# Gathered rows in four PSUM banks, sums three ticks behind, and edge steps set apart in a graph network kernel

## The chip, the cores and the metric

The kernel runs on one core of a Trainium2 chip. The metric is the device time of one execution in microseconds. Three runs of the kernel before gave 4328.02, 4320.78 and 4327.1 us; the median is 4327.1 us. A separate execution under the hardware profiler took 5199.93 us. Instruction times below come from that execution.

## What is computed

Two graph layers over 12,500 nodes with 64 features and 200,000 edges, sorted by `dst`. The first layer is two mean aggregations with weights, the second a small network per edge with a mean by `src`:

```python
def _sage_conv(x, src, dst, Wl, Wr, b):
    agg = jax.ops.segment_sum(x[src], dst, num_segments=N)
    cnt = jax.ops.segment_sum(jnp.ones((src.shape[0],), x.dtype), dst, num_segments=N)
    mean = agg / jnp.maximum(cnt, 1.0)[:, None]
    return mean @ Wl.T + b + x @ Wr.T
...
h = jnp.maximum(_layernorm(x, axis=-1), 0.0)
x = x + conv2(relu(conv1(h)))
h = jnp.maximum(_layernorm(x, axis=-1), 0.0)
# second layer, per edge (senders = src, receivers = dst)
inp = jnp.concatenate([h[senders], h[receivers], edge_attr_64], axis=-1)
msg = jax.nn.relu(inp @ W1 + b1) @ W2 + b2
x = x + _segment_mean(msg, senders, N)
```

`conv1` and `conv2` stand for `_sage_conv` with the two sets of weights.

## The kernel before

Gather and scatter are matrix products. The nodes are cut into 49 blocks of 256, the edges into 49 x 49 = 2401 cells by the block of their two ends, each cell padded to 128 places. A gather multiplies a one-hot matrix (`turned`, 128 places by 256 nodes in two halves) with a block's table of node rows; a sum multiplies another one-hot matrix (`hot`) with the gathered rows. A table keeps each value in three bf16 pieces, so a row has 3 x 64 = 192 columns, and 193 with the count.

The stages, in order:

1. `features` (to about 114 us of the profiled execution): layer norm of the inputs.
2. `cells` (to about 857 us): places the edges of a block in their cells, block by block.
3. The two convolutions (L812 to L825, to about 3713 us, with a drain of some 14 us): a loop over 2 x 601 ticks, each of four cells or the odd one left over.
4. The last stage (L831 on): per-edge messages and their mean, eight cells a tick.

**A tick of the convolutions.** `Line` keeps a list of generators. `line.tick(new)` adds a generator and advances each by one step, the oldest first. `some_cells` (L769) is the generator of four cells: in its first step eight gather products (L775) into `got`, one `hot` on VectorE (L639), and one ScalarE copy (L782) of 768 columns from PSUM to bf16 `rows`; then two yields; then the eight sum products (L664) into `acc`. So TensorE's queue holds, tick after tick, the sums of two ticks ago and then the gathers of this one. When the last cell of a block has been summed, the same generator goes on with `conv` (L700): a ScalarE copy of the sums (L703) in the same step, then the mean and the reassembled own rows on VectorE (L707 to L715), two transposes (L719), a copy (L721), the weights (L725), bias (L727), and `after_conv1` or `after_conv2`, which writes the next tables.

**PSUM** has eight banks. `psum_x` holds two for everything named `pX`, which `conv`, `after_conv2`, `final` and `edge_terms` share. `sums_ps` holds two for `acc` and four for `got`: two buffers of two banks, each for four cells.

**Beside the ticks** runs `edge_terms` (L321), the part of the second layer that needs only the edge attributes. It works in 209 units of mostly four transposes: transpose (L353), ScalarE copy (L355), product with the weights (L361, each recorded as two), ScalarE copy (L364), and up to eight indirect scatters on GpSimd (L369) into the tables `terms` in memory. It is a generator too. `Beside` advances it by counted time: each tick counts 0.37 or 0.375 us a cell, each step costs 10.4/6 us. In the cell stage it is advanced from block 18 on, 2.4 us at each of five places a block. A full unit is six steps: transpose and copy; product; copy and two scatters; two scatters; two; two.

**`tb`** is the table of the second convolution. As `after_conv2` computes the receivers' table for the last stage, it stores each block to `b_mem` (L767), since `tb` is still being gathered; the last two blocks go to `tb` at once. The list `again` (L812) loads `tb` back seven blocks at a time, once they have been gathered for the last time.

The order of every engine's queue is that in which the program writes it (a manual schedule); each engine runs its queue in order.

Of the kernel before, what the change touches and what calls it, by code (L numbers as in the profile page):

```python
# [9 lines left out]
FT = mybir.dt.float32  # L10
# [104 lines left out]
def fast_path(  # L115
# [205 lines left out]
    def edge_terms(work, psum):  # L321

        loads = []
        for q in (*range(BJ - 3), BJ - 1, BJ - 3, BJ - 2):
            blocks = range(q * J, min(q * J + J, NB))
            step = 3 if len(blocks) == J else 4
            loads += [(blocks, t0, min(step, TG - t0)) for t0 in range(0, TG, step)]

        def load(blocks, t0, m):
            n = len(blocks)  # L330
            e = work.tile([P, J, 3, 2 * D], FT, name="edges")
            ev = e.rearrange("p j c d -> p (j c) d").rearrange("p (a c) d -> p a c d", a=n if n == J else 1)
            for i, B in enumerate(blocks):
                s = nc.sync.value_load(begin_i[0:1, B:B + 1], min_val=0, max_val=E - WIN)
                a = edge[bass.ds(s, WIN)].rearrange("(p t) d -> p t d", t=T)
                nc.sync.dma_start(ev[:, i, 0:m].rearrange("p c d -> p (c d)"),
                                  a[:, 2 * t0:2 * (t0 + m)].rearrange("p t d -> p (t d)"))
            return ev

        ahead = load(*loads[0])  # L340
        for at, (blocks, t0, m) in enumerate(loads):
            n = len(blocks)
            ev = ahead

            if n == J:
                units = [[(i, t0 + c, ev[:, i, c]) for i in range(n)] for c in range(m)]
            else:
                units = [[(0, t0 + c, ev[:, 0, c]) for c in range(m)]]
            for u, unit in enumerate(units):
                k = len(unit)  # L350
                pt = psum.tile([P, 4, P], FT, name="pX", bufs=2)
                for c, (_, _, a) in enumerate(unit):
                    nc.tensor.transpose(pt[:, c], a, ident)  # L353
                et = work.tile([P, 4, P], FT, name="edges_t")
                nc.scalar.copy(et[:, :k], pt[:, :k])  # L355
                if u == 0 and at + 1 < len(loads):
                    ahead = load(*loads[at + 1])
                yield
                pm = psum.tile([P, 4, 2, D], FT, name="pX", bufs=2)
                for c in range(k):  # L360
                    nc.tensor.matmul(pm[:, c], et[:, c], we, start=True, stop=True)  # L361
                yield
                o = work.tile([P, 4, 2, D], FT, name="terms_o", bufs=4)
                nc.scalar.copy(o[:, :k], pm[:, :k])  # L364
                for h in range(2):
                    for c, (i, tg, _) in enumerate(unit):
                        B = blocks[i]
                        t = 2 * tg + h
                        nc.gpsimd.indirect_dma_start(  # L369
                            out=terms[B % J][:], out_offset=bass.IndirectOffsetOnAxis(  # L370
                                ap=pos[:, B, t:t + 1], axis=0),
                            in_=o[:, c, h], in_offset=None,
                            bounds_check=EROWS - 1, oob_is_err=False)
                        if c % 2 == 1:
                            yield

    class Beside:

# [314 lines left out]
    psum = ctx.enter_context(tc.tile_pool(name="sums_ps", bufs=2, space=bass.MemoryType.PSUM))  # L693
    sums = Sums(psum)
    layers = ExitStack()
    work = layers.enter_context(tc.tile_pool(name="layers", bufs=2))
    next_rows = rows_with_one(work)
    line = Line()

    def conv(layer, table, w, b, finish, B, acc):  # L700

        v = work.tile([P, 2, W3], FT, name="sums")
        nc.scalar.copy(v, acc[:, :, :W3])  # L703
        yield
        m = work.tile([P, 2, 2, D], FT, name="both")
        t = table[:, B]
        nc.vector.tensor_add(m[:, :, 1], t[:, :, 0:D], t[:, :, D:2 * D])  # L707
        nc.vector.tensor_add(m[:, :, 1], m[:, :, 1], t[:, :, 2 * D:])
        nc.vector.tensor_add(m[:, :, 0], v[:, :, 0:D], v[:, :, D:2 * D])
        nc.vector.tensor_add(m[:, :, 0], m[:, :, 0], v[:, :, 2 * D:D3])  # L710
        if layer == 0:
            c = work.tile([P, 2], FT, name="cnt")
            nc.vector.tensor_scalar(c, v[:, :, D3], 1.0, None, op0=OP.max)
            nc.vector.reciprocal(rcnt[:, B], c)
        nc.vector.tensor_mul(m[:, :, 0], m[:, :, 0], bc(rcnt[:, B], D))  # L715
        yield
        pt = psum_x.tile([P, 4, P], FT, name="pX", bufs=2)
        for h in range(2):
            nc.tensor.transpose(pt[:, h], m[:, h].rearrange("p a d -> p (a d)"), ident)  # L719
        ct = work.tile([P, 2, P], FT, name="both_t")  # L720
        nc.scalar.copy(ct, pt[:, :2])  # L721
        yield
        po = psum_x.tile([P, 8, D], FT, name="pX", bufs=2)
        for h in range(2):
            nc.tensor.matmul(po[:, h], ct[:, h], w, start=True, stop=True)  # L725
        o = work.tile([P, 2, D], FT, name="conv")
        nc.vector.tensor_add(o, po[:, :2], rows(b, 2))  # L727
        yield
        yield from finish(B, o)
# [6 lines left out]
    def after_conv2(B, o):  # L736
# [9 lines left out]
        yield from layernorm_relu(work, h, v, 2)  # L746
        yield
        nc.sync.dma_start(of_block(x2_mem, B), v)
        pt = psum_x.tile([P, 4, P], FT, name="pX", bufs=2)
        nc.tensor.transpose(pt[:, 0], h.rearrange("p h d -> p (h d)"), ident)  # L750
        ht = work.tile([P, P], FT, name="h2_t")
        nc.scalar.copy(ht, pt[:, 0])
        yield
        po = psum_x.tile([P, 4, P], FT, name="pX", bufs=2)
        nc.tensor.matmul(po[:, 0:2], ht, wsr, start=True, stop=True)
        ab = work.tile([P, 2, 2, D], FT, name="ab", bufs=3)
        nc.scalar.copy(ab[:, 0], po[:, 0:2, :D])
        nc.vector.tensor_add(ab[:, 1], po[:, 0:2, D:], rows(bias[2], 2))
        yield
        last = B >= NB - 2  # L760
        b = tb[:, B] if last else work.tile([P, 2, D3], BF, name="b_out", bufs=3)
        for _ in zip_longest(three(work, ta[:, B], ab[:, 0], nc.vector.tensor_sub),
                             three(work, b, ab[:, 1], nc.vector.tensor_sub)):
            yield
        yield
        if not last:
            nc.sync.dma_start(of_block(b_mem, B), b)  # L767

    def some_cells(layer, t, c0, a, z):  # L769
        n = z - a  # L770
        table = (ta, tb)[layer]
        p = psum.tile([P, 2, 512], FT, name="got")
        for c in range(n):
            for h in range(2):
                nc.tensor.matmul(p[:, c // 2, c % 2 * D3:(c % 2 + 1) * D3],  # L775
                                 t[:, h, (a - c0 + c) * S:(a - c0 + c + 1) * S],
                                 table[:, (a + c) % NB, h], start=h == 0, stop=h == 1,
                                 skip_group_check=True)
        o = hot(work, dcol[:, even(a, z)], 4)
        g = next_rows()  # L780
        if n == G:
            nc.scalar.copy(g[:, :, :D3].rearrange("p (a c) d -> p a c d", c=2),  # L782
                           p[:, :, :2 * D3].rearrange("p a (c d) -> p a c d", c=2))
        else:
            for c in range(n):
                nc.scalar.copy(g[:, c, :D3], p[:, c // 2, c % 2 * D3:(c % 2 + 1) * D3])
        yield
        yield
        B = sums.add(o, g, a, z)
# [19 lines left out]
                    pass  # L809


    again = [(s, min(s + CH, NB - 2)) for s in range(0, NB - 2, CH)]  # L812
    todo = [(layer, *p) for layer in range(2) for p in parts(G)]
    for (layer, c0, c1, part), t, coming in ahead(
            todo, lambda p: wait_rows(work, "srow", srow_b, p[1], p[2]),
            lambda p, r: turned(work, "turned", r, p[2] - p[1])):
        for a, z in part:
            line.tick(some_cells(layer, t, c0, a, z))
            next(coming, None)
            beside.passed((z - a) * (0.37, 0.375)[layer])  # L820
            while layer and again and z - (CELLS - NB) >= again[0][1]:
                B0, B1 = again.pop(0)
                nc.sync.dma_start(tb[:, B0:B1],
                                  b_mem[B0 * BLK:B1 * BLK].rearrange("(b p h) d -> p b h d", p=P, h=2))
    line.finish()  # L825
    beside.rest()
    layers.close()
    terms_in.close()


    work = ctx.enter_context(tc.tile_pool(name="last", bufs=2))  # L831

    def final(K, acc):
        v = work.tile([P, 2, W3], FT, name="sums")
# [14 lines left out]
        nc.vector.tensor_mul(o, rows(bias[3], 2), bc(c[:, 2], D))  # L849
        nc.vector.tensor_add(o, o, xv)  # L850
        yield
        pt = psum_x.tile([P, 4, P], FT, name="pX", bufs=2)
        nc.tensor.transpose(pt[:, 0], m.rearrange("p h d -> p (h d)"), ident)
        mt = work.tile([P, P], FT, name="m_t")
        nc.scalar.copy(mt, pt[:, 0])
        yield
        po = psum_x.tile([P, 8, D], FT, name="pX", bufs=2)
        nc.tensor.matmul(po[:, 0:2], mt, wo, start=True, stop=True)
        yield
        nc.vector.tensor_add(o, o, po[:, 0:2])  # L860
# [76 lines left out]
    for (c0, c1, part), (ts, td), coming in ahead(  # L937
            list(parts(G3)), lambda p: (wait_rows(work, "srow", srow_k, p[0], p[1]),
                                        wait_rows(work, "drow", drow_k, p[0], p[1])), turned_both):
        for n, (a, z) in enumerate(part):  # L940
            p = psum.tile([P, G3, 2 * D], FT, name="got")
            line.tick_behind(messages(e, p, ts, td, c0, a, z))
            for _ in range(2):
                next(coming, None)
# [266 lines left out]
```

## Time and profile before

| | |
|---|---|
| median of three runs | 4327.1 us |
| profiled execution | 5199.93 us |
| its span | 5197.9 us |
| mean granted TensorE clock | 0.896 |

The profiled execution is 873 us longer than the median. Shares within it are read stage by stage, and a sum made in it does not carry over to the median one to one.

| engine | busy, us | share of the span |
|---|---|---|
| TensorE products (PE) | 4002.0 | 77% |
| TensorE weight loads (PEld) | 3699.5 | 71% |
| VectorE (DVE) | 3406.1 | 66% |
| GpSimd (POOL) | 2641.4 | 51% |
| ScalarE (ACT) | 2418.3 | 47% |

A group line names the source line, engine, operation and tiles; after the bar stand busy time, the mean of one in ns, the engine's idle time just before the group, and what ended most of it. TensorE overlaps consecutive products, so one product lasts some 250 ns in the records while the next starts about 83 ns later.

### The profile page before, as it was taken

Reading aid. Unit: us, or ns where it says so; the run is one execution under the profiler, and the core shown is the slowest. Engines: PE = TensorE matmul, PEld = TensorE weight load, DVE = VectorE, ACT = ScalarE, POOL = GpSimd, SP = SyncE. Lnnn points to the kernel's source line nnn. Section 1 sums busy time; section 2 is a strip of 40 time slices with the busy share of each in tenths; the row PEclk is TensorE's granted clock in tenths of the full one; section 3 lists DMA queues with packets and bytes.
Section 4 is the critical chain, followed back from the end, with each engine's and each line's share of the span. In section 5 each row is a group of like instructions: output and inputs, shape, how many; then the busy total and the mean of one; then the engine's idle time right before and its main releaser. Section 6 shows DMA issues by size and latency. Waiting matters only on the chain.

```text
span 5197.9 us, 123211 instructions
## 1 busy us (share of the span) xinstructions
PE 4002.0 (77%) x50387; PEld 3699.5 (71%) x50387; DVE 3406.1 (66%) x6079; ACT 2418.3 (47%) x4487; POOL 2641.4 (51%) x2300
## 2 busy tenths in 40 slices
PE   0785674778777877777777776777799999999897
PEld 0454453777777777677777775777788988888897
DVE  6784662555445544455555554555799999999997
ACT  2010112444444444444444443444566776676676
POOL 2047876555445554455455535555255555555554
PEclk9665766999889999899899988999899999999999
DMA  6941212233223222223233232322445544554453
GB/s 230 346 150 33 55 39 71 89 95 93 87 78 95 91 90 78 86 87 103 82 97 95 89 96 76 97 88 86 157 161 177 176 169 165 177 170 165 165 178 113
DMA packets 309518, 620.81 MB, mean 119 GB/s; under 512 B 74402, under 2 KB 158630, under 8 KB 308864
## 3 DMA queue, kind: packets, MB, share of 16 engines
q1 hardware_dynamic: 247572, 557.98, 32.5%
q0 software_dynamic: 53312, 51.36, 3.4%
q8 instruction: 395, 6.47, 0.5%
q10 hardware_dynamic: 8060, 3.53, 0.3%
q14 instruction: 179, 1.47, 0.1%
HBM read 465.04 MB, written 150.96 MB: 119 GB/s over the span
## 4 chain that ended last, share of the span: by engine, by line
PE 49%; issue 14%; DVE 10%; another core or an unknown queue 7%; POOL 7%; ACT 6%; DMA 2%; SPq 0%; POOLq 0%; ACTq 0%; DVEq 0%
PE acc L664 18%; PE got L775 11%; PE got L884 8%; POOL terms L369 7%; PE got L885 4%; ACT rows L782 4%; PE pX L361 3%; DVE turned_d L630 2%; DVE turned L630 1%; DVE hot L639 1%; PE pX L353 1%; DVE y L890 1%; DMA terms<-terms_o,pos 1%; PE pX L725 1%
## 5 line engine op out<-in xcount | busy, mean ns | idle before, releaser
L369 POOL DMA_INDIRECT terms<-terms_o,pos x1666 | 1834.7, 1101 | 1718.7 <-ACT terms_o L364 593.6
L782 ACT CAST rows<-got 128x768 bf16<-128x768 f32 x1200 | 958.4, 801 | 1443.5 <-PE got L775 740.1
L664 PEld LDWEIGHTS <-hot 128*128 128x128 bf16 x12006 | 1110.8, 103 | 360.3 <-issue 332.4
L664 PE MATMUL acc<-rows,hot 128*128 128x193 bf16 x9604 | 1087.7, 259 | 269.7 <-ACT rows L782 229.5
L897 POOL TENSOR_TENSOR hidden<-hidden 128x512 f32<-128x512 f32 (+1 forms) x602 | 771.6, 1282 | 752.9 <-ACT hidden L894 642.7
L630 DVE TENSOR_SCALAR turned<-srow,nid 128x2048 bf16<-128x2048 bf16 (+1 forms) x906 | 749.7, 842 | 334.1 <-PE got L775 139.0
L639 DVE TENSOR_TENSOR hot<-dcol,local 128x1024 bf16<-128x1024 bf16 x1202 | 801.0, 683 | 156.3 <-remote 75.9
L775 PEld LDWEIGHTS <-turned 128*128 128x128 bf16 x9604 | 863.5, 102 | 29.3 <-issue 20.9
L884 PE MATMUL got<-tb,turned_d 128*128 128x128 bf16 x4802 | 755.0, 223 | 83.5 <-DVE turned_d L630 83.5
L884 PE MATMUL got<-ta,turned 128*128 128x128 bf16 x4802 | 743.8, 222 | 23.4 <-DVE y L891 15.9
L885 PE MATMUL got<-tb,turned_d 128*128 128x64 bf16 x4802 | 686.1, 195 | 0.0
L885 PE MATMUL got<-ta,turned 128*128 128x64 bf16 x4802 | 677.8, 195 | 0.0
L775 PE MATMUL got<-ta,turned 128*128 128x192 bf16 x4802 | 531.1, 256 | 9.0 <-issue 8.4
L775 PE MATMUL got<-tb,turned 128*128 128x192 bf16 x4802 | 526.2, 255 | 6.8 <-issue 6.6
L361 PE MATMUL pX<-we,edges_t 128*128 128x128 f32 x1666 | 290.1, 327 | 311.8 <-ACT edges_t L355 203.6
L884 PEld LDWEIGHTS <-turned_d 128*128 128x128 bf16 x4802 | 449.1, 100 | 99.1 <-DVE turned_d L630 95.4
L905 ACT ACTIVATE hot_a<-every,less 128x256 bf16<-128x256 bf16 x1200 | 507.1, 493 | 0.0
L361 PEld LDWEIGHTS pX<-we,edges_t 128*128 128x128 f32 x1666 | 250.9, 230 | 342.4 <-ACT edges_t L355 222.3
L884 PEld LDWEIGHTS <-turned 128*128 128x128 bf16 x4802 | 449.9, 99 | 35.5 <-DVE y L891 27.2
L885 PEld LDWEIGHTS <-turned_d 128*128 128x128 bf16 x4802 | 447.0, 99 | 0.0
L885 PEld LDWEIGHTS <-turned 128*128 128x128 bf16 x4802 | 445.1, 99 | 0.0
L906 ACT ACTIVATE hot_a<-hot_a 128x1024 bf16<-128x1024 bf16 x300 | 317.1, 1057 | 9.5
(207 smaller groups left out, 4944.8 us busy)
## 6 DMA issues: line engine op xcount, KB each, us to landing
srow<-srow_b SPq DMA_DIRECT2D x300, 512.0 KB
terms<-zero SPq DMA_DIRECT2D x96, 832.0 KB
srow<-srow_k SPq DMA_DIRECT2D x150, 512.0 KB
drow<-drow_k SPq DMA_DIRECT2D x150, 512.0 KB
terms_in<-terms SPq DMA_DIRECT2D x147, 384.0 KB
edges<-in_edge_attr_dram SPq DMA_DIRECT2D x240, 192.0 KB
terms<-terms_o,pos POOLq DMA_INDIRECT x1666
terms_in<-terms SPq DMA_DIRECT2D x49, 416.0 KB
```

What stands on the lines that cost most here:

```text
L361: nc.tensor.matmul(pm[:, c], et[:, c], we, start=True, stop=True)
L369: nc.gpsimd.indirect_dma_start(out=terms[B % J][:], out_offset=bass.IndirectOffsetOnAxis(ap=pos[:, B, t:t + 1], axis=0), in_=o[:, c, h], i ...
L630: nc.vector.tensor_scalar(o[:, h, :n * S], r[:, :n * S], nid[:, h:h + 1], None, op0=OP.is_equal)
L639: nc.vector.tensor_tensor(o[:, :n], cols.rearrange("p (g c) -> p g c", c=2).unsqueeze(2).to_broadcast([P, n, 2 * P, 2]), local.rearrange(" ...
L664: nc.tensor.matmul(self.acc[B][:, h, :W3], lt, r[:, c, 0:W3], start=k + h == 0, stop=k == NB - 1 and h == 1, skip_group_check=True)
L775: nc.tensor.matmul(p[:, c // 2, c % 2 * D3:(c % 2 + 1) * D3], t[:, h, (a - c0 + c) * S:(a - c0 + c + 1) * S], table[:, (a + c) % NB, h], s ...
L782: nc.scalar.copy(g[:, :, :D3].rearrange("p (a c) d -> p a c d", c=2), p[:, :, :2 * D3].rearrange("p a (c d) -> p a c d", c=2))
L884: nc.tensor.matmul(p[:, c], lt, rt[:, 0:2 * D], start=i == 0, stop=False, skip_group_check=True)
L885: nc.tensor.matmul(p[:, c, 0:D], lt, rt[:, 2 * D:], start=False, stop=i == 3, skip_group_check=True)
L897: nc.gpsimd.tensor_sub(w[:, :n, (i + 1) * D:(i + 2) * D], w[:, :n, j], upper(w)[:, :n, j])
L905: nc.scalar.activation(q[:, c - k], every, AF.Abs, bias=less[(a + c) // NB][:, (a + c) % NB:(a + c) % NB + 1])
L906: nc.scalar.activation(q[:, :n - k], q[:, :n - k], AF.Relu, bias=1.0, scale=-2.0)
```

## The change

- `some_cells` takes a pair of cells at a time: four gather products into a tile of one bank, then a ScalarE copy of 384 columns. The tile has four buffers, in a pool of its own (`gather_ps`), closed after the convolutions.
- A third yield stands before the sums, and `hot` gets five buffers instead of four.
- `conv` begins with a yield, so its ScalarE copy of the sums comes one tick after them.
- `pX` keeps one bank for the node side; `edge_terms` has its own, `pE`.
- In `edge_terms` each operation has a step of its own: transpose; copy; nothing; product; nothing; copy. The scatters form a generator `scatter`, of which two are issued in each of the four middle steps of the next unit.
- The reload of `tb` is decided as the program is written: which blocks have been gathered for the last time, which are stored, which are present.
- The last stage's `got` gets a pool of its own with the same two buffers; its operations stay.

```diff
+        def scatter(o, blocks, unit):
+            for h in range(2):
+                for c, (i, tg, _) in enumerate(unit):
+                    B = blocks[i]
+                    t = 2 * tg + h
+                    nc.gpsimd.indirect_dma_start(
+                        out=terms[B % J][:], out_offset=bass.IndirectOffsetOnAxis(
+                            ap=pos[:, B, t:t + 1], axis=0),
+                        in_=o[:, c, h], in_offset=None,
+                        bounds_check=EROWS - 1, oob_is_err=False)
+                    if c % 2 == 1:
+                        yield
+        before = iter(())
...
-                pt = psum.tile([P, 4, P], FT, name="pX", bufs=2)
+                pt = psum.tile([P, 4, P], FT, name="pE")
                 for c, (_, _, a) in enumerate(unit):
                     nc.tensor.transpose(pt[:, c], a, ident)
-                et = work.tile([P, 4, P], FT, name="edges_t")
-                nc.scalar.copy(et[:, :k], pt[:, :k])
                 if u == 0 and at + 1 < len(loads):
                     ahead = load(*loads[at + 1])
                 yield
-                pm = psum.tile([P, 4, 2, D], FT, name="pX", bufs=2)
+                et = work.tile([P, 4, P], FT, name="edges_t")
+                nc.scalar.copy(et[:, :k], pt[:, :k])
+                next(before, None)
+                yield
+                next(before, None)
+                yield
+                pm = psum.tile([P, 4, 2, D], FT, name="pE")
                 for c in range(k):
                     nc.tensor.matmul(pm[:, c], et[:, c], we, start=True, stop=True)
+                next(before, None)
                 yield
+                next(before, None)
+                yield
+                for _ in before:
+                    pass
                 o = work.tile([P, 4, 2, D], FT, name="terms_o", bufs=4)
                 nc.scalar.copy(o[:, :k], pm[:, :k])
-                for h in range(2):
...
+                before = scatter(o, blocks, unit)
+                yield
+        for _ in before:
+            pass
...
+    gather = layers.enter_context(tc.tile_pool(name="gather_ps", bufs=4, space=bass.MemoryType.PSUM))
...
     def conv(layer, table, w, b, finish, B, acc):
 
+        yield
         v = work.tile([P, 2, W3], FT, name="sums")
         nc.scalar.copy(v, acc[:, :, :W3])
...
-        pt = psum_x.tile([P, 4, P], FT, name="pX", bufs=2)
+        pt = psum_x.tile([P, 4, P], FT, name="pX")
...
-        last = B >= NB - 2
+
+        last = gathered[0] > B
         b = tb[:, B] if last else work.tile([P, 2, D3], BF, name="b_out", bufs=3)
+        if last:
+            present.add(B)
...
             nc.sync.dma_start(of_block(b_mem, B), b)
+            stored.add(B)
...
     def some_cells(layer, t, c0, a, z):
         n = z - a
         table = (ta, tb)[layer]
-        p = psum.tile([P, 2, 512], FT, name="got")
-        for c in range(n):
-            for h in range(2):
-                nc.tensor.matmul(p[:, c // 2, c % 2 * D3:(c % 2 + 1) * D3],
...
-        o = hot(work, dcol[:, even(a, z)], 4)
         g = next_rows()
-        if n == G:
-            nc.scalar.copy(g[:, :, :D3].rearrange("p (a c) d -> p a c d", c=2),
-                           p[:, :, :2 * D3].rearrange("p a (c d) -> p a c d", c=2))
...
+        for c in range(0, n, 2):
+            m = min(2, n - c)
+            p = gather.tile([P, 512], FT, name="got")
+            for i in range(c, c + m):
+                for h in range(2):
+                    nc.tensor.matmul(p[:, (i - c) * D3:(i - c + 1) * D3],
+                                     t[:, h, (a - c0 + i) * S:(a - c0 + i + 1) * S],
+                                     table[:, (a + i) % NB, h], start=h == 0, stop=h == 1,
+                                     skip_group_check=True)
+            nc.scalar.copy(g[:, c:c + m, :D3], p[:, :m * D3].rearrange("p (c d) -> p c d", c=m))
+        o = hot(work, dcol[:, even(a, z)], 5)
+        yield
         yield
         yield
         B = sums.add(o, g, a, z)
...
-    again = [(s, min(s + CH, NB - 2)) for s in range(0, NB - 2, CH)]
+    gathered, stored, present = [0], set(), set()
+
+    def again():
+        new = [B for B in range(gathered[0]) if B in stored and B not in present]
+        if new and (len(new) >= CH or not line.all):
+            B0 = new[0]
+            B1 = next(B for B in range(B0, NB + 1) if B not in new or B == B0 + CH)
+            nc.sync.dma_start(tb[:, B0:B1],
+                              b_mem[B0 * BLK:B1 * BLK].rearrange("(b p h) d -> p b h d", p=P, h=2))
+            present.update(range(B0, B1))
+            return True
...
-            while layer and again and z - (CELLS - NB) >= again[0][1]:
-                B0, B1 = again.pop(0)
...
+            if layer:
+                gathered[0] = max(z - (CELLS - NB), 0)
+                again()
     line.finish()
+    while again():
+        pass
...
+    gather = ctx.enter_context(tc.tile_pool(name="last_ps", bufs=2, space=bass.MemoryType.PSUM))
...
-            p = psum.tile([P, G3, 2 * D], FT, name="got")
+            p = gather.tile([P, G3, 2 * D], FT, name="got")
```

More of the change, by code (lines that the diff above doesn't have):

```diff
@@ L358, in edge_terms @@
                 yield
-                pm = psum.tile([P, 4, 2, D], FT, name="pX", bufs=2)
+                et = work.tile([P, 4, P], FT, name="edges_t")
[5 more added lines that the diff above has]
+                pm = psum.tile([P, 4, 2, D], FT, name="pE")
                 for c in range(k):
                     nc.tensor.matmul(pm[:, c], et[:, c], we, start=True, stop=True)
+                next(before, None)
                 yield
+                next(before, None)
+                yield
+                for _ in before:
+                    pass
                 o = work.tile([P, 4, 2, D], FT, name="terms_o", bufs=4)
                 nc.scalar.copy(o[:, :k], pm[:, :k])
-                for h in range(2):
[L366 to L375, printed above, removed]
+                before = scatter(o, blocks, unit)
+                yield
+        for _ in before:
+            pass
     class Beside:
@@ L722, in conv @@
         yield
-        po = psum_x.tile([P, 8, D], FT, name="pX", bufs=2)
+        po = psum_x.tile([P, 8, D], FT, name="pX")
         for h in range(2):
@@ L748, in after_conv2 @@
         nc.sync.dma_start(of_block(x2_mem, B), v)
-        pt = psum_x.tile([P, 4, P], FT, name="pX", bufs=2)
+        pt = psum_x.tile([P, 4, P], FT, name="pX")
         nc.tensor.transpose(pt[:, 0], h.rearrange("p h d -> p (h d)"), ident)
@@ L753, in after_conv2 @@
         yield
-        po = psum_x.tile([P, 4, P], FT, name="pX", bufs=2)
+        po = psum_x.tile([P, 4, P], FT, name="pX")
         nc.tensor.matmul(po[:, 0:2], ht, wsr, start=True, stop=True)
@@ L771, in some_cells @@
         table = (ta, tb)[layer]
-        p = psum.tile([P, 2, 512], FT, name="got")
-        for c in range(n):
-            for h in range(2):
[L775 to L778, printed above, removed]
-        o = hot(work, dcol[:, even(a, z)], 4)
-        g = next_rows()
-        if n == G:
-            nc.scalar.copy(g[:, :, :D3].rearrange("p (a c) d -> p a c d", c=2),
-                           p[:, :, :2 * D3].rearrange("p a (c d) -> p a c d", c=2))
-        else:
-            for c in range(n):
-                nc.scalar.copy(g[:, c, :D3], p[:, c // 2, c % 2 * D3:(c % 2 + 1) * D3])
+        g = next_rows()
+        for c in range(0, n, 2):
[10 more added lines that the diff above has]
+        yield
         yield
@@ L820, in fast_path @@
             beside.passed((z - a) * (0.37, 0.375)[layer])
-            while layer and again and z - (CELLS - NB) >= again[0][1]:
-                B0, B1 = again.pop(0)
-                nc.sync.dma_start(tb[:, B0:B1],
-                                  b_mem[B0 * BLK:B1 * BLK].rearrange("(b p h) d -> p b h d", p=P, h=2))
+            if layer:
+                gathered[0] = max(z - (CELLS - NB), 0)
+                again()
     line.finish()
+    while again():
+        pass
+    assert present == set(range(NB))
     beside.rest()
@@ L851, in final @@
         yield
-        pt = psum_x.tile([P, 4, P], FT, name="pX", bufs=2)
+        pt = psum_x.tile([P, 4, P], FT, name="pX")
         nc.tensor.transpose(pt[:, 0], m.rearrange("p h d -> p (h d)"), ident)
@@ L856, in final @@
         yield
-        po = psum_x.tile([P, 8, D], FT, name="pX", bufs=2)
+        po = psum_x.tile([P, 8, D], FT, name="pX")
         nc.tensor.matmul(po[:, 0:2], mt, wo, start=True, stop=True)
```

## The prediction

> **What bounds it now.** The page comes first, for the stages. The chain that ended last is half TensorE, and its largest pieces are the sums and the gathers of the two convolutions.
>
> ```profile
> span 5197.9 us, 123211 instructions
> ...
> PE 49%; issue 14%; DVE 10%; another core or an unknown queue 7%; POOL 7%; ACT 6%; DMA 2%; SPq 0%; POOLq 0%; ACTq 0%; DVEq 0%
> PE acc L664 18%; PE got L775 11%; PE got L884 8%; POOL terms L369 7%; PE got L885 4%; ACT rows L782 4%; PE pX L361 3%; DVE turned_d L630 2%; DVE turned L630 1%; DVE hot L639 1%; PE pX L353 1%; DVE y L890 1%; DMA terms<-terms_o,pos 1%; PE pX L725 1%
> ```
>
> The windows view cut at the stages (first to last gather: 857.6 to 3711 us): length; busy time of PE, PEld, DVE, ACT, POOL with counts; granted clock; DMA share; GB/s. The cell stage, the two convolutions, the short tail after the edges' terms have ended, the last stage:
>
> ```profile
> 114.00:857.00 743.00, 471.18 (x4278) 335.85 (x4278) 467.89 (x701) 80.77 (x231) 409.71 (x326) 0.67 0.37 123
> 857.00:2268.00 1411.00, 1093.12 (x10905) 1034.21 (x10906) 704.91 (x1385) 626.14 (x1011) 726.61 (x684) 0.91 0.28 88
> 2268.00:3641.00 1373.00, 1041.90 (x10335) 976.93 (x10333) 742.67 (x1698) 628.93 (x1214) 687.76 (x647) 0.91 0.30 92
> 3641.00:3713.00 72.00, 63.67 (x694) 60.63 (x692) 50.74 (x121) 41.49 (x81) 10.66 (x11) 0.95 0.41 124
> 3713.00:5198.00 1485.00, 1327.37 (x24167) 1290.11 (x24166) 1372.57 (x2068) 1011.65 (x1915) 771.62 (x602) 0.97 0.50 166
> ```
>
> The last stage leaves PE 11% idle and is not touched. The convolutions leave it 23% idle, ACT 55%, DVE 48%: nothing is full, so they wait for each other. For whom, the groups of the page say (after the bar: busy time, mean ns, idle time before them, what ended it):
>
> ```profile
> L782 ACT CAST rows<-got 128x768 bf16<-128x768 f32 x1200 | 958.4, 801 | 1443.5 <-PE got L775 740.1
> L664 PE MATMUL acc<-rows,hot 128*128 128x193 bf16 x9604 | 1087.7, 259 | 269.7 <-ACT rows L782 229.5
> L361 PE MATMUL pX<-we,edges_t 128*128 128x128 f32 x1666 | 290.1, 327 | 311.8 <-ACT edges_t L355 203.6
> ```
>
> The timeline of the tail shows a tick with nothing in its way (start, length): eight sums, eight gathers, 1.33 us.
>
> ```profile
> 3701.44 0.82 PE L775 MATMUL got<-tb,turned 128*128 128x192 bf16 x8
> 3702.10 0.84 PE L664 MATMUL acc<-rows,hot 128*128 128x193 bf16 x8
> 3702.77 0.82 PE L775 MATMUL got<-tb,turned 128*128 128x192 bf16 x8
> ```
>
> Measured from gather to gather in the trace, the 1200 ticks last 2852 us, mean 2.38. The 654 without other PE work have median 1.33, mean 1.68; the 128 that hold an edge unit's four transposes have a tenth percentile of 1.77 and a median of 2.29; the 128 with its eight products 2.25 and 3.72. If every kind of tick took its tenth percentile, the 1200 would take **1915 us**: about what PE's own work needs. The excess is 937 us.
>
> Why PE waits: the copy L782 should start when the eighth gather is done. Against the later of that and ACT's previous end it starts a median 0.09 us late, but over 0.3 us late in 448 of 1200, 910 us in all. What delays it no record names; in the tail, without edge terms, the ticks run at 1.33. PE's gaps between 857 and 3713 us, weight loads included, add up to 660 us: 269 before L664 (196 times, mean 1.4), 187 before L361 (89 times, 2.1), 185 before the node side's matmuls (L719 76, L725 46, L755 38, L750 26), the rest small.
>
> **Part by part.**
>
> *Sums three ticks behind, banks one by one.* Today the sums of tick t-2 open PE's tick t. Between the end of gather t-2 and that moment PE has one tick, 1.33 us; the copy needs 0.80 and some 0.2 for the two hand-overs. Slack about 0.33 us, which the late copies (p75 1.24, p90 2.43) exceed. With one more tick it is 1.66. The ring of banks must allow it: the first pair of gather t needs its bank back from t-2; its copy can start after four gathers, so between lie 0.33 + 1.33 + 0.67 = 2.33 us against 0.48 and hand-overs, slack about 1.65 as well. The 196 gaps before L664 average 1.4, so most vanish and the long ones lose 1.33: of 269 I leave 80, **-190**. Late next is the same copy, when it is over 1.66 late.
>
> *Two copies for one.* ACT gets 1200 more instructions. The nearest row is `sums<-acc` L703, also PSUM to SBUF with 386 columns, mean 491 ns, median 482; two are 0.96 against 0.80: +0.16 a tick, +196 us of ACT. Here the Trainium skill speaks against the change: "Perfetto Trace Analysis", Optimizing Scalar/DVE Operations, advises larger operations, as each pays an access overhead; "ScalarE: Activation LUTs", What ACT_TABLE_LOAD costs, gives 186 ns + 0.833 ns per column, so 2 x 506 against 826: +0.19 a tick, an estimate of +223 us. Either would end in the time only were ACT full. ACT works 1412 us in 857-3713; with 196 it has 1608 of at least 1915, so I cost it at nothing; the cover is 0.25 us a tick, and a rival below takes it away.
>
> *Edge steps apart.* A unit keeps six steps. Transposes, ACT copy and products now have a step between copy and products, where L361 stood one step behind copy and transposes. A step is 1.73 us of counted time, 1.2 ticks. Of 187 us before L361 I leave 40: **-147**. The eight scatters come behind the next unit's copy, two in a step as before; POOL's 1666 scatters keep their 1.06 us and 0.30 us of issue, 1800 us for 1321 in the convolutions, under PE's floor. They end later by at most a unit: the code counts 36 x 5 x 2.4 + 2401 x 0.745 = 2221 us of due time, 1281 steps, against 1254 needed, so about 30 ticks remain; in the trace the last scatter starts at 3653.4, the first load of terms at 3729.7. Nothing.
>
> *Convolution sums a tick later.* ACT no longer stands at L703 for PE (31 us idle) with the row copies queued behind. DVE gets its input earlier relative to PE, but six operations of 0.29 still lie ahead of L719. One bank for the node side: its next write already needs the reader of the last, ticks before. Of 185 I take **-50**; bounds +30 (the shared bank bites) and -120.
>
> *Rest.* The fifth `hot` buffer only lets DVE run ahead. At the turn of the layers block 48 is ready 11 ticks after its last gather instead of 9 and is read at 13: hidden, 2 ticks of cover. On SP the loads of `tb` stay 7 and the stores 47, one load a tick at most; what stands behind them is the last x rows. The drain of 14 us after 3713 is a chain of single operations, not of ticks. The last stage's tiles take the same four banks. Zero, at most 3 us each way.
>
> *Clock.* At 0.91 granted, with two levels, 18% of the convolutions run at half speed: 491 us in 96 periods, in which 1806 of 19208 sums and gathers start, each about 80 ns longer: 145 us. "TensorE: Matmul & The Clock Gate", What's actually happening, lets the clock fall after an idle window of about 3.4 us. Only 38 gaps are that long (206 us); by it only the longest count, 38 x 3.4 us at half speed, some 65 us, and the change, which shortens gaps by 1.3, would win perhaps 30. The trace shows 96 periods, so shorter gaps add up too. I take half of 145: **-70**.
>
> Sum in the profiled execution: 190 + 147 + 50 + 70 = 457 of the 937 excess, 49%. **5200 would become about 4740.**
>
> To the median: 4327 is 873 below the profiled execution. The cell stage has an excess too: its 48 intervals between blocks last 650 us, at the commonest 9.1 they would last 437: 213. Floor: 5200 - 937 - 213 = 4050. The median lies 277 above it, 24% of the 1150. Shared evenly, the convolutions' excess is 226 in an unprofiled run. Short waits are covered more fully than long ones, so I take 60% rather than 49%: -136; and of the cells' 51, where products stand behind their copy likewise (L361 waits 96 us there), -16. **4327 - 152 = 4175.**
>
> **Rivals.**
>
> *All of it goes* (0.18): without profiling the waits are under 1.6 us and the slack covers them all. For: 75% of the late copies are under 1.24. Against: DVE before L719 stays. -226 and half the cells' 51: 4075.
>
> *The lateness is PE's own* (0.17): if the matmuls end late rather than their news arriving late, slack moves the wait. For: ACT and DVE often resume within 0.1 us of each other after PE. Against: the gaps lie only before instructions that wait, hardly ever within a group. Left are L703's wait and some of L361: 35 us, 4292.
>
> *ACT becomes the bound* (0.08), slower. Each half copy waits for PE on its own. ACT's work is 1.34 a tick; the excess-scaled lateness is 910 x 0.24 / 1200 = 0.18 a copy. If both halves pay it, 1.70 a tick, still under today's (1915 + 226)/1200 = 1.78. It decides from 0.22 a half; at 0.26, 1.86 and +95: 4420. Against: halves in a row share one delay.
>
> *Nothing changes* (0.04): the waits go to POOL's scatters, whose next copy ACT must serve: 4325.
>
> **Numbers.** Mine has 0.53, 4110 to 4245. Faster: 0.53, 0.18 and most of 0.17, in all 0.85; same 0.04; slower 0.11 (ACT, and the turn or the shared bank going wrong). A measurement tells 0.2%, 9 us, from no change. The range takes in the full gain and the small one: 4050 to 4300.
>
> **What would show it.** Right: L361's idle time below 100 us; L664's below 100; two casts of 128x384 at about 480 ns; tick mean near 2.0; clock above 0.93; the last stage within 10 us of 1485. Wrong: idle time before L664 ended by PE or its queue, or before L775 by ACT; ACT over 75% busy in the convolutions; the first terms load held by scatters.

## The result, and the profile after

| | before | changed |
|---|---|---|
| median of the timed runs | 4324.56 us (14) | 4313.22 us (14) |
| ratio, 95% interval | | 0.9973, 0.9965 to 0.9981 |
| profiled execution | 5199.93 us | 4318.44 us |

The change wins 11 us, 0.27%, where 152 were forecast; 4313 lies outside the range of 4050 to 4300. The last row is the second surprise: the profiled execution of the changed kernel takes as long as its timed runs, while that of the kernel before was 20% longer than its own.

The page of the changed kernel: span, chain by engine and by line, the scatters, and the row copies and sums that answer to those shown of before (after the bar: busy time, mean ns, idle time before, what ended most of it).

```profile
span 4316.5 us, 124949 instructions
...
PE 54%; issue 12%; DVE 11%; POOL 10%; DMA 4%; ACT 2%; SPq 1%; POOLq 0%; ACTq 0%; DVEq 0%
PE acc L681 20%; PE got L801 13%; POOL terms L345 10%; PE got L919 10%; PE got L920 5%; DMA terms<-terms_o,pos 3%; PE pE L380 3%; DVE turned_d L647 3%; DVE turned L647 2%; DVE hot L656 1%; PE pE L368 1%; DVE y L925 1%; DVE mean L880 1%; PE pX L744 1%; ACT rows L805 1%
...
L345 POOL DMA_INDIRECT terms<-terms_o,pos x1666 | 1898.3, 1139 | 803.0 <-issue 462.9
L805 ACT CAST rows<-got 128x384 bf16<-128x384 f32 x2402 | 1035.5, 484 | 578.8 <-PE got L801 568.4
...
L681 PE MATMUL acc<-rows,hot 128*128 128x193 bf16 x9604 | 1008.8, 247 | 2.2 <-DVE hot L656 2.2
```

The sums (now L681) waited 2.2 us in all, where L664 had waited 270; the products of the edges (now L380) never waited in the convolutions. The windows view by stage (length; busy PE, PEld, DVE, ACT, POOL with counts; granted clock; DMA share; GB/s), cut at the first gather, the last scatter and the last sum:

```profile
127.00:806.80 679.80, 474.23 (x4194) 340.93 (x4194) 456.57 (x683) 79.83 (x230) 390.60 (x303) 0.70 0.38 126
806.80:2802.50 1995.70, 1924.03 (x21696) 1892.65 (x21697) 1474.12 (x3161) 1350.28 (x3464) 1507.67 (x1364) 0.99 0.41 128
2802.50:2827.20 24.70, 21.39 (x242) 20.10 (x239) 16.08 (x42) 14.48 (x42) 0.01 (x1) 1.00 0.69 205
2827.20:4316.00 1488.80, 1329.10 (x24168) 1291.38 (x24168) 1373.72 (x2068) 1013.01 (x1916) 771.45 (x602) 0.97 0.50 166
```

Read on its own against the first profile of before, this would look like a triumph: the convolutions fell from 2855 to 2020 us. The timed runs say that nothing of the kind happened, so it was the first profile that had to be looked at again.

### The profile page after: what moved, and what is told of

The parts are those of the page before. It is cut to its first block, busy times and chain, and to the rows that moved or that the text cites. A ratio compares the mean times of both kernels' runs of the same rounds, so it can differ in the third digit from the quotient of the medians.

```text
span 4316.5 us, 124949 instructions
## 1 busy us (share of the span) xinstructions
PE 3760.4 (87%) x50387; PEld 3550.8 (82%) x50387; DVE 3400.7 (79%) x6079; ACT 2487.0 (58%) x5687; POOL 2704.7 (63%) x2300
## 4 chain that ended last, share of the span: by engine, by line
PE 54%; issue 12%; DVE 11%; POOL 10%; DMA 4%; ACT 2%; SPq 1%; POOLq 0%; ACTq 0%; DVEq 0%
PE acc L681 20%; PE got L801 13%; POOL terms L345 10%; PE got L919 10%; PE got L920 5%; DMA terms<-terms_o,pos 3%; PE pE L380 3%; DVE turned_d L647 3%; DVE turned L647 2%; DVE hot L656 1%; PE pE L368 1%; DVE y L925 1%; DVE mean L880 1%; PE pX L744 1%; ACT rows L805 1%
## 5 line engine op out<-in xcount | busy, mean ns | idle before, releaser
L345 POOL DMA_INDIRECT terms<-terms_o,pos x1666 | 1898.3, 1139 | 803.0 <-issue 462.9
L805 ACT CAST rows<-got 128x384 bf16<-128x384 f32 x2402 | 1035.5, 484 | 578.8 <-PE got L801 568.4
L681 PEld LDWEIGHTS <-hot 128*128 128x128 bf16 x12006 | 1045.9, 99 | 46.3 <-issue 30.5
L681 PE MATMUL acc<-rows,hot 128*128 128x193 bf16 x9604 | 1008.8, 247 | 2.2 <-DVE hot L656 2.2
L801 PEld LDWEIGHTS <-turned 128*128 128x128 bf16 x9604 | 813.2, 98 | 7.5 <-issue 6.3
L801 PE MATMUL got<-ta,turned 128*128 128x192 bf16 x4802 | 495.4, 246 | 6.1 <-issue 5.8
L801 PE MATMUL got<-tb,turned 128*128 128x192 bf16 x4802 | 496.8, 247 | 0.0
L919 PEld LDWEIGHTS <-turned 128*128 128x128 bf16 x4802 | 450.6, 99 | 35.3 <-DVE y L926 27.3
L920 PEld LDWEIGHTS <-turned 128*128 128x128 bf16 x4802 | 445.7, 99 | 0.0
L647 DVE TENSOR_SCALAR turned_d<-drow,nid 128x2048 bf16<-128x2048 bf16 (+1 forms) x302 | 309.7, 1068 | 1.9 <-DMA drow<-drow_k 1.9
L929 ACT ACTIVATE hidden<-y 128x512 f32<-128x512 f32 (+1 forms) x301 | 190.0, 631 | 206.2 <-DVE y L926 190.8
```

The lines of the kernel that those rows point to most:

```text
L345: nc.gpsimd.indirect_dma_start(out=terms[B % J][:], out_offset=bass.IndirectOffsetOnAxis(ap=pos[:, B, t:t + 1], axis=0), in_=o[:, c, h], i ...
L647: nc.vector.tensor_scalar(o[:, h, :n * S], r[:, :n * S], nid[:, h:h + 1], None, op0=OP.is_equal)
L681: nc.tensor.matmul(self.acc[B][:, h, :W3], lt, r[:, c, 0:W3], start=k + h == 0, stop=k == NB - 1 and h == 1, skip_group_check=True)
L801: nc.tensor.matmul(p[:, (i - c) * D3:(i - c + 1) * D3], t[:, h, (a - c0 + i) * S:(a - c0 + i + 1) * S], table[:, (a + i) % NB, h], start=h ...
L805: nc.scalar.copy(g[:, c:c + m, :D3], p[:, :m * D3].rearrange("p (c d) -> p c d", c=m))
L919: nc.tensor.matmul(p[:, c], lt, rt[:, 0:2 * D], start=i == 0, stop=False, skip_group_check=True)
```

## The experiments

The prediction's theory was that TensorE (PE) waits for the row copies and the edge copy. Against it stood two others: that those waits belonged to one profiled execution (theory A below), and that the indirect scatters on GpSimd's queue hold the pace in both kernels (theory P).

**The kernel before, profiled again** (no edit).

> The kernel before, profiled a second time. Theory A (its first profile was slowed by something that the timed runs do not have): the span is near 4325 us, the convolutions take about 2030 us instead of 2855, the row copies start within 0.1 us of the gathers and L664 and L361 wait under 60 us together. Theory B (this kernel's order is open to a disturbance that profiling always brings, the changed one is not): the span is again near 5200 us, with some 250 us of idle time before L664.

Measured: 4315.69 us profiled. The same windows of this execution:

```profile
127.00:805.60 678.60, 468.97 (x4203) 344.49 (x4203) 456.41 (x684) 77.77 (x230) 387.74 (x304) 0.70 0.38 127
805.60:2788.80 1983.20, 1906.28 (x21491) 1873.05 (x21492) 1462.36 (x3126) 1272.20 (x2254) 1488.96 (x1363) 0.99 0.41 127
2788.80:2829.80 41.00, 38.64 (x441) 37.18 (x438) 31.54 (x77) 26.36 (x52) 0.00 (x0) 1.00 0.55 165
2829.80:4313.00 1483.20, 1327.06 (x24167) 1289.49 (x24166) 1370.65 (x2068) 1011.73 (x1915) 771.00 (x602) 0.97 0.49 166
```

The convolutions take 2024 us, PE is busy for 96% of them, the clock is at 0.99. Two groups of its page, which waited 1443 and 270 us in the first profile:

```profile
L782 ACT CAST rows<-got 128x768 bf16<-128x768 f32 x1200 | 958.3, 799 | 659.6 <-PE got L775 639.2
L664 PE MATMUL acc<-rows,hot 128*128 128x193 bf16 x9604 | 1008.9, 247 | 11.1 <-ACT rows L782 11.0
```

Of 1200 row copies 3 start over 0.3 us late, against 448; PE's gaps in the convolutions add up to 78 us, against 660. Before L361 there are none in the convolutions; its 82.9 us lie in the cell stage. Theory A holds: what the change was built to remove in my account was hardly there.

**A third profile of before, and a second of the changed kernel** (no edits), to see whether the 5200 us come back.

> The kernel before, profiled a third time. If the slow first execution was an accident: 4310 to 4335 us and fewer than 20 row copies over 0.3 us late. If this kernel falls into it often: near 5200 us again.

> The changed kernel, profiled a second time. If the slow execution was an accident of one run: 4300 to 4325 us, PE's gaps in the convolutions under 100 us as before. If profiling can bring it to either kernel: over 4400 us.

Measured: 4324.33 and 4303.23 us. One profile of three of before took 5200 us, none of two of the changed kernel, and none of those of the eleven edited kernels below: an accident as far as seen; its cause stays open. With two clean profiles of each kernel the 11 us can be placed. First gather to last sum: 2024 and 2032 us before, 2020 and 2006 after, 15 less in the mean. Cell stage: 679 and 680 against 680 and 679, nothing. From the last sum on: 1484 and 1483 against 1489 and 1489, 5 more; part of that is the drain to the first gather of the last stage, 20 and 20 us before, 22 and 22 after. Two profiles each are few, and the spread within a kernel (8 and 14 us in the convolutions) is about as large as the difference.

**No scatters at all.** In both kernels the indirect scatter is left out and the tables keep their zeros.

```diff
-                        nc.gpsimd.indirect_dma_start(
...
```

> The kernel before without the 1666 indirect scatters of the edges' terms; the tables keep their zeros, so the last stage adds zeros. Theory P (POOL's scatters at 1.46 us apart set the pace of the convolutions in both kernels): the convolutions fall to PE's 1915 us and the cell stage by 50 to 150, in all 4080 to 4180 us, and the same time as the changed kernel without scatters. Theory Q (PE's own work sets it): 4270 to 4325 us.

> The changed kernel without the 1666 indirect scatters; the tables keep their zeros. Theory P: PE's last 100 us of waiting go, convolutions 1915 to 1935 us, in all 4070 to 4170 us. Theory Q: 4270 to 4313 us.

Measured: 4132.36 us (ratio to before 0.9565, 0.955 to 0.958) and 4109.22 us (0.9503, 0.9488 to 0.9519). Theory P gave the size of the totals. Its split was half right. The cell stage and the convolutions of before without scatters:

```profile
127.00:665.00 538.00, 421.92 (x4202) 307.85 (x4202) 449.57 (x683) 80.42 (x231) 0.00 (x0) 0.75 0.41 142
665.00:2646.00 1981.00, 1936.92 (x21927) 1905.01 (x21928) 1469.28 (x3203) 1298.02 (x2304) 0.00 (x0) 1.00 0.34 110
```

The cell stage falls from 679 to 538 us, but the convolutions only from 2024 to 1981. So most of what the queue costs is in the cell stage; in the convolutions PE is nearly full beside it. And without the queue the two kernels differ by 23 us, twice what they differ by with it: part of what the change wins is hidden behind the scatters.

**Half the scatters.** In the changed kernel the scatters of the second half of each pair are left out; those terms stay zero.

```diff
-            for h in range(2):
+            for h in range(1):
```

> The changed kernel with the scatters of the first half of each pair alone (833 of 1666), so half the terms stay zero. Theory P: 833 x 1.46 = 1216 us of queue no longer fill the 2500 us there are, nearly all of the 204 us that no scatters save come back: 4105 to 4140 us. Theory C, each scatter costs its share: 4200 to 4220 us.

Measured: 4118.68 us (0.9519). Half the scatters give back 195 of the 204 us that all of them cost. A price per scatter would have given half; a queue that is full with 1666 and not with 833 would give nearly all.

Where it is full, the trace of before (second profile) shows in the cell stage, in its view of waits from 320 to 805 us (who waited for whom: total us, times, longest):

```profile
ACT terms_o L364 <- DMA terms<-terms_o,pos: 224.6, 29, 11.7
POOL terms L369 <- ACT terms_o L364: 224.2, 2, 223.9
ACT rows_o L565 <- PE pC L562: 97.3, 28, 5.6
PEld pX L361 <- ACT edges_t L355: 92.2, 31, 9.4
```

ACT's copy of the finished terms needs a buffer, and its four buffers are still waiting to be scattered. While ScalarE (ACT) stands there, the copies of the cell stage stand behind it. (The second row is GpSimd's idle time before its very first scatter.) GpSimd's own waits from 250 to 2800 us:

```profile
POOL terms L369 <- issue: 464.9, 1500, 2.9
POOL terms L369 <- ACT terms_o L364: 232.2, 7, 223.9
POOL terms L369 <- DMA terms<-terms_o,pos: 84.2, 87, 4.5
```

From its first scatter at 325.6 to the end of the last at 2788.8 the queue runs 2463 us: 1877 busy in scatters of 1.13 us and, by estimate, some 508 in the 0.305 us between one scatter and the next (1665 times), 97% together. The page shows POOL at 62%: that is a share of the whole span, and the time between scatters counts as idle (busy time alone is 76% of the 2463 us).

**More buffers for the copied terms**, in both kernels.

```diff
-    o = work.tile([P, 4, 2, D], FT, name="terms_o", bufs=4)
+    o = work.tile([P, 4, 2, D], FT, name="terms_o", bufs=12)
```

> The changed kernel with 12 buffers for the copied terms instead of 4. Theory P (the GpSimd queue is full from its first scatter to its last, and in the cell stage it pushes back through the four buffers on ACT, 225 us of waiting of the terms copy for old scatters): the cell stage falls from 680 towards 540 us, the convolutions follow at once, and the end comes when 1666 scatters at 1.46 us are through, 324 + 2427 = 2751 us plus some 30 instead of 2827: 4240 to 4280 us. Theory C (scatters disturb the other engines by contention, not by the queue): 4305 to 4318 us.

> The kernel before with 12 buffers for the copied terms instead of 4. Theory P: about the same time as the changed kernel with 12 buffers, within 15 us (the scatter queue is the bound of both), 4245 to 4295 us. Theory C: 4315 to 4330 us.

Measured: 4271.31 us (0.9872, 0.9856 to 0.9887) and 4275.02 us (0.9881, 0.9866 to 0.9896). Twelve buffers win 51 us in the kernel before and 42 in the changed one, and with them the change is worth 4 us, within the spread. The windows of the changed kernel with twelve buffers:

```profile
127.00:727.00 600.00, 443.18 (x4194) 318.82 (x4194) 453.34 (x682) 79.61 (x230) 327.78 (x239) 0.74 0.42 140
727.00:2729.00 2002.00, 1940.59 (x21935) 1909.75 (x21935) 1490.00 (x3203) 1364.65 (x3504) 1514.95 (x1379) 0.99 0.42 130
2729.00:2800.00 71.00, 4.42 (x20) 2.10 (x17) 8.73 (x33) 4.62 (x17) 48.36 (x50) 0.53 0.19 53
2800.00:4264.00 1464.00, 1324.59 (x24153) 1289.23 (x24151) 1363.71 (x2036) 1007.36 (x1899) 771.72 (x602) 0.97 0.50 167
```

The cell stage is 79 us shorter (600 us, where 540 had been expected), the convolutions end at 2729, and then for 71 us every engine but GpSimd is nearly idle: 50 scatters are left, and the last stage does not begin before them. PE's last product before it and its first gather in this execution:

```profile
2741.97 1.22 PE L774 MATMUL pX<-wsr,h_t 128*128 128x256 f32 x2 [0.35 <-ACT h_t L771]
2798.70 0.27 PE L919 MATMUL got<-ta,turned 128*128 128x128 bf16 x1 [55.51 <-DMA drow<-drow_k]
```

The queue's own end hardly moved (2802.5 to 2792.3, where 2751 had been expected); what was won is the work that used to follow it. What holds the last stage back is not the load of the terms: its very first load, of the cells' rows (`srow`, L637), already waits 49.2 us for scatters on SyncE's queue. The program closes the pool of the scattered buffers (`terms_in.close()`) just before it makes these tiles, so they may get that memory; no run tested this.

**Scatters earlier**, on top of the twelve buffers: once in the changed kernel, once with the edge steps of before.

```diff
-        CLEAR = 18
+        CLEAR = 15
```

> The changed kernel with 12 buffers for the copied terms and the edge steps begun at block 15 of the cell stage instead of 18. Theory P (the scatter queue is full from its first entry on): the first scatter comes up to 25 us earlier than 326, held back only by the clearing of the tables, whose last write is issued at 294.6, and the end follows it: 4245 to 4262 us. If something else now ends last: 4266 to 4275 us.

> The same with the edge steps in the order of before and two shared banks (gather side of the change alone, 12 buffers, begun at block 15). If the edge steps apart cost time, as the run with them alone suggests (6 us): 3 to 10 us under the run beside it. If the scatter queue hides them: the same within 4 us.

Measured: 4272.49 us (0.9879) and 4271.77 us (0.9867). A miss: in the changed kernel the first scatter came 17 us earlier, at 309.1, but the queue took 2487 us instead of 2466 and ended at 2796. Why it slowed is not settled. The edge steps make no difference here that can be told.

**The parts of the change alone.** The gather side (pairs, four banks, third tick, later copy of the sums, the reload) with the edge steps of before; the edge steps with their own bank alone; the one yield alone, whose edit is shown.

```diff
     def conv(layer, table, w, b, finish, B, acc):
+        yield
         v = work.tile([P, 2, W3], FT, name="sums")
```

> The changed kernel with the edge steps as they were before (transpose and copy in one step, scatters right behind the second copy, two shared banks): so the pairs of cells in four banks, the third tick, the later copy of the sums and the reload alone. If the gather side carries the gain: 4310 to 4316 us. If the edge steps carry it: 4321 to 4328 us. If PE's waits of the first profile were real in the timed runs: under 4250 us.

> The kernel before with the edge steps of the change alone (each operation in a step of its own, scatters a unit later, a bank of its own for the edges and one for the node side); gathers, sums and conv as before. In the second profile of before L361 never waited, so these steps have nothing to win: 4318 to 4328 us. If they carry a part of the gain all the same: 4312 to 4318 us. If the single edge bank costs (transposes behind a copy that waits for old scatters): 4328 to 4340 us.

> The kernel before with the one yield ahead of the copy of the sums, nothing else. If the later copy of the sums is what the change wins by (ACT no longer stands at the sums with the row copies queued behind it): 4313 to 4318 us. If it is the banks and the third tick: 4322 to 4328 us.

Measured: gather side 4315.53 us (0.9982, 0.9975 to 0.9989), edge steps 4332.28 us (1.0013, 1.0006 to 1.002), the yield 4331.48 us (1.0008, 0.9999 to 1.0017, no difference that can be told, and above both expected ranges). The gather side alone wins 8 of the 11 us; the edge steps alone cost some 6 (3 to 9). These do not add up to the whole: together the parts win 11, not 2. The trace of the edge steps names a new wait in the convolutions, of the weight loads of the transposes:

```profile
PEld pE L368 <- ACT terms_o L388: 53.4, 117, 13.6
```

With one bank for the edges the next unit's transposes need the copy of the terms, and that copy may be standing behind old scatters. So the full queue now reaches PE through the bank: without scatters this cost is nearly gone, as the table shows. It splits PE's time in the convolutions by what came next: for each product the time from the start of the product before it to its own start, summed in us.

| | gathers | sums | edge transposes | edge products | node side |
|---|---|---|---|---|---|
| before (second, third profile) | 795, 795 | 848, 847 | 69, 69 | 148, 148 | 163, 172 |
| changed (two profiles) | 796, 796 | 837, 834 | 102, 91 | 150, 150 | 135, 136 |
| gather side alone | 806 | 837 | 68 | 148 | 162 |
| edge steps alone | 794 | 834 | 122 | 150 | 138 |
| before, no scatters | 793 | 833 | 68 | 148 | 138 |
| changed, no scatters | 792 | 832 | 71 | 150 | 124 |

So the 15 us are a balance: in the mean the sums take 12 us less and the node side 32 less, and the edge transposes 28 more. The edge steps alone win about as much at the sums and the node side (44 us), and lose 53 at the transposes, so their cost of some 6 us is what is left of the two. With one profile of each part this is a reading, not a test, and no run parts the edges' own bank from their new steps.

**The gather side without scatters**; the tables keep their zeros.

> The gather side of the change alone (edge steps as before), without the 1666 scatters; the tables keep their zeros. With the queue out of the way the two parts add up: before without scatters took 4132, the whole change 4109. If the gather side carries it all: 4105 to 4113 us. If the edge steps carry it: 4125 to 4135 us.

Measured: 4120.20 us (0.9525), between the two expectations: without the queue the gather side and the edge steps share the gain, 12 and 11 us as the times stand, 17 and 10 by the ratios to before, whose intervals are 6 to 9 us to either side.

## Why the prediction was wrong, point by point

- **The floor of a tick.** Right: in a clean trace too the tenth percentiles of the tick kinds add up to 1914 us (changed kernel).
- **What bounds.** Wrong: "nothing is full, so they wait for each other". The scatter queue is 97% full from its first entry to its last. I read POOL's 51% and costed its 1800 us as "under PE's floor"; with VectorE beside it a scatter comes every 1.46 us, 1363 x 1.46 = 1990 us in the convolutions, and in the cell stage it is asked for more than it can do. Yet the queue is not all that holds the convolutions: without it they are only 43 us shorter, 1981. PE itself is busy for 96% of them in the second profile; the first, with 77%, hid that.
- **The step that failed: the way from the profiled execution to the median.** I saw that the median was 873 us shorter, and spread what was left, 277 us, evenly over the stages: 226 us to the convolutions, 51 to the cells. In the second profile of before the 1200 ticks take 2021 us, 106 above the floor, and the 48 block intervals 625, 188 above theirs. Most of the excess was in the stage that the gather side doesn't touch. Then 60% of the 226, 136 us, was to go; of the 106 the change took 15, and PE's gaps only went from 78 to 74 us. The four terms of the sum had failed before any sharing, because they were read from waits that this kernel mostly does not have: before L664 PE waited 11 us and not 269, before L361 not at all in the convolutions and not 187, before the node side 66 and not 185 (45 in the changed kernel), and half speed lasted some 40 us of the convolutions and not 491.
- **Two copies for one.** Right: 484 ns each against 482 forecast (the shortest of L703's copies; their median is 487), and hidden. The cost to ACT was put too high: 1365 us busy in the convolutions, not 1608. The 1412 us of before added durations that overlap in the records (the windows show 1297), and the copies overlap again: 2402 of 484 ns would be 1163 us end to end and are 1035.5.
- **Edge steps apart.** Wrong in sign: forecast -147 in the profiled execution, measured +6 alone. What the trace shows in its place was costed at nothing: the transposes' wait for their single bank, behind a copy that old scatters hold up (69 to 122 us in the table). What the steps did win, at the node side and the sums, was not forecast of them.
- **Later copy of the sums.** Forecast -50 in the profile with bounds +30 and -120; alone 0.0008 slower with zero in the interval.
- **Clock.** Forecast -70. In the first profile 38 gaps of PE are over 3.4 us and 96 periods of half speed begin, in the second 3 and 3. That shorter gaps add up, as the prediction read from the first, the second does not show.
- **Rivals.** The nearest was the one with the smallest chance, that the waits go to the scatters and nothing changes (4325, 0.04). Its number is near by luck in part: the waits did not move, they were hardly there; but the scatters that ACT must wait for are what it named. That all of the excess goes (4075) fell with the 226 us. That ACT becomes the bound is refuted: its row copies take 77 us more of busy time (1035.5 against 958.3) and the sums waited 2 us. That the matmuls themselves end late was not tried; its case fell with the first profile.
- **A misread line.** The lateness of p75 1.24 and p90 2.43 us is that of all 1200 row copies, not of the late ones: of the 448 late, half are over 1.7 us and a quarter over 2.5. Even in the first profile the slack of 1.66 us would not have covered half of them.
- **What was to show it.** Nearly all signs of "right" came true (sums waiting 2 us, casts at 484 ns, clock 0.99, last stage 1489; only the ticks came out at 1.68 where 2.0 was named), and none of "wrong". Apart from the two casts they would have been true of before as well, so they could not tell the two apart.

## What to carry to other kernels

When a profiled execution is far from the timed runs, its waits are not a budget: the excess can't be shared out over the stages by rule, so bound the gain by what the timed run can hold, stage by stage, before pricing a single wait. Count a queue as full by its pitch times its entries, with the time between entries, and look for the stage where the buffers in front of it run out; a deeper ring there was worth 51 us in the kernel before, where a finer pipeline beside it was worth 11. A shared or single buffer turns a full queue into a wait of an engine that has nothing to do with it.

## What the hardware showed

A scatter of 128 rows takes 0.973 us when no instruction of VectorE overlaps it (114 in the changed kernel's convolutions; as long when ScalarE is busy, 101 of them) and 1.15 us in the mean when only a `hot` comparison does (180); where nothing holds it up, the next follows 0.305 us after its end. Overlap alone does not decide it: 50 that overlapped a `hot` and an addition into `conv` took 0.973 us too. At the mean of 1.139 us the excess adds up to 0.166 x 1666 = 277 us of the queue, an estimate of what VectorE costs it if all of the excess is due to overlap; PE's gaps in the convolutions are 74 us in all.

A profiled execution of the same program can be 20% longer than the next: there a quarter of the row copies started over 1.2 us after the last gather's recorded end and ACT's own last instruction, against none over 0.4 us in the second profile, and 96 periods of half clock began in the convolutions instead of 3.
